# One column of ones beside each head's values, a fifth key and value tile, unread products in TensorE's gaps, and a new list of due times

## The chip, the cores and the metric

The kernel runs on one core of one Trainium2 chip. The metric is device microseconds (us) of one execution; the time of a kernel is the median of several runs. TensorE is written PE (its weight loads PEld), VectorE DVE, ScalarE ACT, GpSimd POOL and SyncE SP. All data is float32.

## The reference

Sixteen batches of 256 rows with 256 channels go through two blocks, 16 heads of 16 channels each. Cut to what matters:

```python
m = silu(mod) @ w_ada + b_ada                    # nine rows of shift, scale and gate per batch
h = ln(x) * (1 + sc_msa) + sh_msa                # self attention in windows of 128, rolled by 64
x = x + self_attn(h) * g_msa
h = ln(x) * (1 + sc_mca) + sh_mca                # cross attention to a context of 256 rows
scores = einsum('bqhd,bkhd->bhqk', q, k) / 4
top_s, top_i = top_k(scores, 16)                 # only the 16 largest scores of 256 are kept
x = x + (softmax(top_s) applied to v[top_i]) @ w_co * g_mca
h = ln(x) * (1 + sc_mlp) + sh_mlp
x = x + (silu(h @ w_a) * (h @ w_b) @ w_m2) * g_mlp     # hidden size 1024
# second block: x is the query, the context is normalised, shifted and scaled; plain attention
out = x + softmax(q k / 4) v @ Wp + bp
```

## The kernel before, in words

The work of one batch is cut into operations, each on one engine: a group of matmuls that fill one bank of PSUM, an activation over a bank, a vector operation, or a set of DMAs. `Plan.op` (line 195) only records them. Every operation has a due time from the table `DUE` (line 33): a whole number for the batch plus thousandths from the list of its stage. The stages are `start` (weights and conditioning), `self`, `prep` (context and queries of the cross attention), `topk`, `mlp` and `last` (the second block); the first two batches, and the last two, have lists of their own. `Plan.order` (line 231) sorts all operations by due time, lets none be due before what it depends on, and that sorted list is the program: each engine executes its operations in that order, SP its DMAs too. A small model of times in the same function serves one purpose in the kernel before, the choice of a buffer among those that will be free. `SWITCH` holds what the model adds where PE changes between its three ways of working: whole array (128), four tiles of 32 rows (32: scores) and four tiles of 32 columns (33: weighted values). `ISSUE`, `BEGIN`, `LAND`, `RATE` describe its DMAs.

In the middle of the run the due times overlap the batches: while batch b is in its cross attention, batch b+1 is in its self attention and batch b-1 in its feed forward and second block. Only the first batches (nothing earlier to overlap with) and the last one differ. Batch 15 is split in two halves of 128 rows from its self attention on (`SPLIT`).

Names and lines that matter below:

- PE transposes an image of normalised rows (line 449), multiplies by weights (475, 511, 558, 888, 915), makes the scores (780 and 788 self, 827 cross, 932 and 944 second block) and the weighted values (581, in `weighted`).
- Lines 661 to 749 make the shift, scale and gate rows of the conditioning. Line 703, in `ada_columns`, multiplies a block of weights by `condT`, 16 columns, one for each batch. Line 724 multiplies a bias by a weight.
- DVE finds the top 16 in two rounds of eight: MAX8 and MATCH_REPLACE8 at lines 846 and 854, then 866 and 871. It also finds row maxima (588), transposes blocks of 32 (538, 548) and divides (540).
- POOL multiplies exponentials with the kept places (875), ACT makes the exponentials (859, 612) and copies out of PSUM (497, 514, 528).
- `lower` (592) sends row maxima from one partition layout to another with eight small DMAs per half (line 605), on SP's queue.
- A value tile `v` holds for each head 16 channels and then 16 columns of ones (line 336), 32 columns in all (`NW`); the product at line 581 so makes the weighted values and, sixteen times over, the sum of the weights. Only the first of the sixteen sums is read, at line 540. The PSUM tiles are `W`, eight banks.

Of the kernel before, what the change touches and what calls it, by code (L numbers as in the profile page):

```python
# [12 lines left out]
ALU = mybir.AluOpType  # L13
# [3 lines left out]
P = 128  # L17
# [11 lines left out]
NW = 32  # L29
# [5 lines left out]
        -3027, -4397, -3471, -3599, -5098, -3376, -2645, -3084, -3618, -1977, -2570, -3085, -3359, -3247, -5174,  # L35
        -3588, -3596, -431, -695, -157, 8, -3035, -3444, -156, -402, -441, -3589, -3159, -3051, -3086, -3323, 86,
        -376, 159, 26, -148, 29, -158, 334, 377, 516, -136, -3437, 524, -402, 345, -448, 430, 1141, 1178, 1253, 540,
        1078, 1334, 228, -58, 443, -404, 1252, -71, 428, 1557, -57, 507, 841, 302, 299, 483, -230, -210, 96, -72,
        1354, 1417, 985, 1558, 1602, 445, 168, -27, 1258, 1342,
    ),  # L40
    "self0": (
        178, -1268, -3395, -1437, -1529, -1439, -5228, -2475, -56, -5103, -2746, -2747, -5249, -2746, -2706, -2925,
        -2729, -5250, -3573, -3327, -3037, -3016, -3187, -3023, -3039, -2555, -3040, -3039, 43, 140, -202, -1119,
        -1116, -910, -811, 145, -81, -38, -132, 17, 157, -1137, -808, -1336, -976, 254, -472, -362, -105, -363, 431,
        -718, -93,
    ),
    "prep0": (
        -2332, -1084, -15, -1103, -1963, 736, -1918, 514, 308, -228, -1334, -1335, 632, -769, 127, 694, -742,
    ),
    "topk0": (  # L50
        629, -11, 508, -65, -2495, -66, 291, 102, -772, 48, 291, 30, -776, 38, 290, 51, -2533, 90, 49, 468, 67, -2304,
        71, 30, 677, 698, -2305, 24, 93, -61, 708, -2254, 674, 702, -38, 789, -2249, 917, 909, 1267, 743, 1295, -125,
        63, -46, 39, -774, 42, -109, 705, -2577, 778, -97, 749, -2266, 745, -98, 745, -2463, 664, 654, 550, 850,
        -2335, 892, 809, -179, 967, -2308, 757, 903, -180, 969, -2327, 908, 719, -196, 1029, 681, 1073, 1237, 1296,
        847, 1335, 924, 961, 1061, 1120, 904, 914, 986, 1120, 686, 985, 978, 983, 924, 992, 1088, 787, 548, 1160, 893,
        998, 1181, 899, 1120, 1159, 1138, 1206, 1183, 998, 1008, 1106, 1004, 838, 1212, 950, 1085, 1192, 781, 1207,
        1244, 1255, 1232, 1293, 1161, 1159, 982, 890, 1096, 782, 1049, 1224, 900, 1184, 933, 1240, 894, 1216, 1140,
        1231, 886, 1224, 1217, 1032, 1206, 737, 1227, 1216, 752, 1198, 738, 1221, 1262, 858, 1287, 848, 1200, 1233,
        783, 1224, 810, 1326, 1299, 1222, 711, 1338, 723, 1099, 849, 1380,
    ),  # L60
    "self1": (
        -3478, -4042, -805, -510, -4612, -2278, -2316, -2237, -4112, -2262, -390, -1118, -3568, -3569, -1018, -2976,
        -3569, -395, -2322, -692, -1489, -1465, -682, -1456, -353, -1219, -1461, -1477, -1495, -1344, -161, -627,
        -165, -3303, -3251, -3334, -3335, -47, -57, 32, 68, 101, -299, -2850, -3108, -3088, -3253, -247, -186, 6,
        -1156, 83, -18, -16, 128,
    ),
    "prep1": (
        -4084, -4257, -17, 53, 102, -42, -411, 147, 218, 181, 36, 33, 206, -260, 510, 225, 282,
    ),
    "topk": (  # L70
        94, 53, 163, 160, 4, 121, -38, 55, -63, 145, -59, 66, 184, 59, -366, 67, 109, 463, -23, 372, 645, 559, 48,
        269, -313, 408, -161, 248, 353, 281, 408, -99, 373, -12, 392, 487, -206, 659, 476, 675, 182, 715, 463, -23,
        499, -47, -199, -24, 504, 82, 263, -22, 545, -475, 2, -451, 531, -453, 268, -421, -453, 561, 667, 565, 225,
        -487, 599, 775, 405, 592, 438, 668, 782, 652, -599, 692, 711, 781, 421, 836, 643, 846, -287, 927, 656, 739,
        712, 799, 836, 747, 417, 768, 859, 606, -19, 673, 566, 625, 195, 477, 684, 541, 942, 30, 1043, 790, 757, 902,
        26, 1047, 722, 784, 775, 756, 905, 863, 693, 718, 757, 907, 775, 1097, 1077, 1166, 825, 1182, 849, 956, 790,
        947, 751, 946, 791, 945, 879, 915, -152, 1008, 1103, 943, 792, 993, 874, 992, 1055, 390, 1120, 1069, 979, 955,
        -104, 1070, 1107, 1011, 972, 968, 1130, 1088, 993, 1010, 633, 1117, 1113, 1176, 1065, 1114, 964, 1201, 391,
        1238, 706, 1108,
    ),  # L80
    "self": (
        -1722, -443, -1198, -804, -2008, -1876, -1546, -1510, -950, -1210, -765, -667, -1033, -1065, -675, -624,
        -1069, -679, -1276, -593, -1090, -1091, -1115, -1012, -430, -1599, -1523, -1474, -1475, -1556, -865, -440,
        -308, -386, -445, -600, -603, -212, -219, -461, -1332, -185, -208, -478, -361, -315, -362, -158, -384, -446,
        -1376, -94, -423, -188, -953,
    ),
    "prep": (
        -23, 5, -310, -291, 112, 73, 257, -32, -1133, -1111, -1134, -3, -291, 405, 25, -209,
    ),
    "last": (  # L90
        1047, 1071, 1127, 1163, 1124, 1206, 712, 1303, 932, 999, 1381, 866, 2035, 1757, 1739, 1723, 2103, 2108, 2222,
        2149, 1885, 2182, 2205, 2121, 1997, 2108, 2080, 2268, 1996, 2015, 2066, 2065, 2014, 2284, 2287, 2028, 2226,
        1991, 2271, 2366, 2356, 2353, 2354, 2141, 1901, 2213, 2403, 1838, 1963, 2116, 2117, 2437, 2000, 2148, 2379,
        2458, 1833, 2404, 1968, 1877, 2530, 2091, 1631, 2565, 1630, 2532, 2446, 2359, 1777, 2068, 2559, 1500, 1410,
        2598, 2600, 2353, 2406, 2302, 2304, 2658, 2404, 2403, 2194, 2680, 2764, 2475, 2722, 2485,
    ),
    "mlp": (
        1494, 1306, 703, 702, 1361, 1433, 838, 1532, 1486, 1250, 1255, 1513, 1352, 1542, 1571, 1599, 1480, 869, 876,
        1488, 1420, 1529, 1359, 1415, 1520, 1197, 863, 1541, 1052, 1568, 1365, 1567, 1554, 1160, 1057, 1670, 1621,
        1724, 1029, 1709, 1814, 1620, 1616, 1553, 1150, 633, 1853, 1121, 1875, 1826, 1793, 1880, 1776, 869, 1898, 941,  # L100
        1609, 1300, 1303, 1625, 1530, 1560, 1531, 1525, 1829, 947, 932, 1677, 1535, 625, 1615, 624, 1989, 1963, 1766,
        1664, 893,
    ),
    "self15": (
        -1970, -648, -1706, -864, -1672, -2110, -1485, -1035, -2085, -1469, -710, -1217, -976, -689, -810, -1331,
        -670, -962, -412, -567, -648, -649, -677, -545, -509, -518, -239, -893, -998, -432, -907, -216, -458, -322,
        -1198, -169, -191, -594, -651, -564, -606, -158, -189, -224, -1271, -89, -174, -108, -1155, -2020, -1743,
        -493, -117, -97, -514, -47, -175, -176, -85, -148, -226, 106, 111, 32, 9, -666, -439, -29, -481, -571, -549,
        253, 149, -73, 249, -74, 317, 269, 257, 330, 323, 162, 60, -269, -4, 69, 211, 72, -4, 335, 413, 434, -56, 352,
    ),  # L110
    "prep15": (
        -81, -120, 34, -136, -399, 69, -211, -438, -39, -1166, -1149, 17, -568, -1106, 38, -400, 459, 424, 409, 523,
        9, 546, 533, 14,
    ),
    "topk15": (
        56, -306, 25, 48, 170, -288, -9, -86, 110, 142, 112, 97, 206, -87, -313, -87, 122, -241, 178, 233, 297, 268,
        152, 238, 161, 510, -5, 154, 322, 369, 534, 580, 153, 151, 106, 269, 215, 671, -599, 572, 189, 878, 421, 389,
        377, 441, 88, 404, 251, 461, 73, 489, 390, 507, 589, 157, 364, -324, -18, 360, 490, -68, 738, 554, 513, 534,
        578, 832, 559, 505, -196, 599, 743, 650, 535, 499, 563, 652, -223, 1019, 1046, 1048, 420, 1209, 601, -563,
        -608, 726, 1012, -512, -647, -604, 898, -605, 551, -517, 984, 745, 436, 884, -224, 763, 575, 340, 1090, 997,  # L120
        -677, 920, 398, 1144, 1115, 972, 782, 454, 1116, 1148, 831, 863, -1632, 1114, 1162, 1194, 1272, 498, 473,
        1296, 1040, 1022, 362, 880, 1006, 963, 452, 1229, 1234, 993, 476, 989, 1113, 1042, 435, 1169, 1195, 990, 981,
        423, 1117, 1009, 1223, 410, 579, 1334, 835, 1047, 1087, 363, 1359, 1297, 1249, 461, 706, 1356, 1052, 1417,
        1140, 1200, -360, 990,
    ),
    "last15": (
        -1505, 17, -219, 55, 280, 1060, 1078, 1157, 1267, 1164, 1161, 1306, 483, 994, 987, 629, 1631, -1051, 1973,
# [51 lines left out]


class Op:
    __slots__ = ("tag", "eng", "cost", "hold", "own", "kb", "emit", "due", "mode", "takes", "uses", "after", "start", "end", "n")


class Plan:
# [910 lines left out]
```

## Time and profile before

| | |
|---|---|
| runs | 1363.39, 1363.4 and 1395.84 us, median 1363.4 |
| the profiled execution | 1365.2 us, of which its span (first to last instruction) is 1363.1 |
| mean granted PE clock | 0.981 of full speed |
| busy in the span | PE 97%, PEld 76%, DVE 89%, ACT 74%, POOL 75% |
| from 220 to 1180 us, each 80 us | PE 79.5 to 80.0 busy, DVE 75.4 to 76.1 |
| first batch's first cross scores (line 827) | 58.2 us |
| last batch's first cross scores | 1208.7 us |

PE's busy time is modelled, because its matmuls are pipelined; a start of one matmul to the start of the next tells more than its length. A matmul of float32 shows as two records here, a transpose as one.

### The profile page before, as it was taken

The numbers are of one execution on the slowest core, as the hardware profiler recorded it, in microseconds if no ns is written. First come the engines' busy times: TensorE is split into PE (matmuls) and PEld (weight loads), VectorE is DVE, ScalarE is ACT, GpSimd is POOL, SyncE is SP. The second block draws the span as 40 slices with busy tenths as digits, with TensorE's granted clock in tenths as the row PEclk, the third lists the DMA queues.
The fourth block names the chain that finished last, engine by engine and source line by source line (L and its number), as shares of the span: only waits on it lengthen the run. The fifth ranks groups of instructions, "written<-read, shape, count | busy, mean of one in ns | idle before, by whom it ended". The sixth has DMA issues, their size and how long they took to land.

```text
span 1363.1 us, 38514 instructions
## 1 busy us (share of the span) xinstructions
PE 1327.1 (97%) x13464; PEld 1040.8 (76%) x13464; DVE 1216.9 (89%) x4357; ACT 1014.4 (74%) x2359; POOL 1026.4 (75%) x1552
## 2 busy tenths in 40 slices
PE   8699999999999999999999999999999999999996
PEld 6466787878778787877878787787878777787875
DVE  3699999999999999999999999999999999998734
ACT  4256778877777878777787878778787877877773
POOL 2456887878788787878878787787878787878752
PEclk9788999999999999999999999999999999999998
DMA  5412000101000010100001010001101000000000
GB/s 158 147 53 58 18 25 18 40 18 41 16 20 25 19 40 18 41 17 18 25 22 37 17 41 18 18 25 22 36 18 41 25 18 25 26 2 10 10 2 18
DMA packets 64161, 42.44 MB, mean 31 GB/s; under 512 B 37764, under 2 KB 56752, under 8 KB 63712
## 3 DMA queue, kind: packets, MB, share of 16 engines
q1 hardware_dynamic: 63967, 39.99, 10.9%
q8 instruction: 107, 1.75, 0.5%
q14 instruction: 87, 0.70, 0.2%
HBM read 35.14 MB, written 4.29 MB: 29 GB/s over the span
## 4 chain that ended last, share of the span: by engine, by line
PE 87%; DVE 5%; POOL 2%; DMA 2%; SPq 1%; issue 1%; ACT 1%; ACTq 0%; POOLq 0%; DVEq 0%
PE W L888 17%; PE W L475 11%; PE W L581 11%; PE W L525 8%; PE W L915 7%; PE W L511 6%; PE W L558 6%; PE W L944 5%; PE W L932 5%; PE W L827 5%; PE W L449 3%; PE W L788 3%; PE W L780 2%; DVE rest L854 1%; DVE rest L871 1%
## 5 line engine op out<-in xcount | busy, mean ns | idle before, releaser
L875 POOL TENSOR_TENSOR prT<-rest,prT 128x512 f32<-128x512 f32 x256 | 325.7, 1273 | 63.5 <-DVE rest L871 49.8
L859 ACT ACTIVATE prT<-W,ntop 128x256 f32<-128x256 f32 x512 | 216.8, 510 | 76.0 <-POOL ntop L848 64.3
L588 DVE TENSOR_REDUCE nm<-W 128x2 f32<-128x512 f32 (+1 forms) x384 | 236.9, 681 | 28.1 <-PE W L932 16.0
L888 PE MATMUL W<-xT,w_L_xcond_w_m 128*128 128x256 f32 (+1 forms) x1088 | 249.0, 375 | 1.5 <-ACT xT L463 1.5
L612 ACT ACTIVATE pTO<-W 128x512 f32<-128x512 f32 (+1 forms) x392 | 200.5, 613 | 62.0 <-PE W L944 37.6
L888 PEld LDWEIGHTS W<-xT,w_L_xcond_w_m 128*128 128x128 f32 x1088 | 189.1, 190 | 57.0 <-ACT pTO L612 10.9
L854 DVE MATCH_REPLACE8 rest<-top,W 128x256 f32<-128x256 f32 x512 | 208.2, 416 | 0.2 <-issue 0.2
L871 DVE MATCH_REPLACE8 rest<-top,rest 128x256 f32<-128x256 f32 x512 | 205.5, 409 | 0.0
L846 DVE MAX8 top<-W 128x8 f32<-128x256 f32 x512 | 187.0, 417 | 14.7 <-PE W L827 14.5
L866 DVE MAX8 top<-rest 128x8 f32<-128x256 f32 x512 | 187.3, 410 | 0.0
L525 PE MATMUL W<-ident,prT 128*128 128x128 f32 x1024 | 144.4, 279 | 11.1 <-POOL prT L875 11.1
L528 ACT ACTIVATE pTT<-W 128x512 f32<-128x512 f32 x256 | 148.4, 621 | 8.8 <-PE W L525 8.7
L541 POOL TENSOR_TENSOR on<-tr,rec 128x128 f32<-128x128 f32 (+1 forms) x162 | 71.0, 443 | 98.6 <-DVE rec L540 98.2
L525 PEld LDWEIGHTS W<-ident,prT 128*128 128x128 f32 x1024 | 120.3, 143 | 32.6 <-POOL prT L875 14.6
L905 POOL TENSOR_TENSOR mb<-ma,mb 128x256 f32<-128x256 f32 (+1 forms) x136 | 94.7, 697 | 62.7 <-ACT mb L903 50.6
L538 DVE STREAM_TRANSPOSE tr<-W 128x256 f32<-128x256 f32 (+1 forms) x162 | 79.2, 490 | 48.1 <-PE W L581 40.1
L915 PE MATMUL W<-w_L_xcond_w_m,h 128*128 128x256 f32 x512 | 113.8, 380 | 0.0
L581 PE MATMUL W<-pTO,v 128*32 128x128 f32 (+1 forms) x2112 | 108.1, 329 | 2.3 <-ACT pTO L612 2.0
L915 PEld LDWEIGHTS W<-w_L_xcond_w_m,h 128*128 128x128 f32 x512 | 95.9, 190 | 13.6 <-POOL prT L875 0.8
L908 POOL TENSOR_TENSOR h<-h,mb 128x256 f32<-128x256 f32 (+1 forms) x136 | 94.8, 697 | 8.3
L581 PEld LDWEIGHTS W<-pTO,v 128*32 128x32 f32 x2112 | 57.8, 111 | 42.6 <-ACT h L907 10.2
L903 ACT ACTIVATE mb<-W,half 128x256 f32<-128x256 f32 (+1 forms) x136 | 69.6, 513 | 9.7 <-PE W L888 8.4
(126 smaller groups left out, 2675.2 us busy)
## 6 DMA issues: line engine op xcount, KB each, us to landing
gate<-gates SPq DMA_DIRECT2D x48, 256.0 KB
q<-nmT SPq DMA_DIRECT2D x480, 1.0 KB
cx<-in_ctx_dram SPq DMA_DIRECT2D x19, 256.0 KB
cx<-in_ctx_dram SPq DMA_DIRECT2D x104, 32.0 KB
rest<-in_L_xcond_w_ada_dram SPq DMA_DIRECT2D x9, 256.0 KB
x<-in_x_dram SPq DMA_DIRECT2D x16, 128.0 KB
x<-in_x_dram SPq DMA_DIRECT2D x32, 64.0 KB
w_L_xcond_w_m<-in_L_xcond_w_m_dram SPq DMA_DIRECT2D x1, 2048.0 KB
```

What stands on the lines that cost most here:

```text
L525: nc.tensor.transpose(w.t[:, ts(n, P)], flat[:, ts(n, P)], ident)
L581: nc.tensor.matmul(po.t[ds(NW * j, NW), ds(q0, nq)], v.t[:, kt, 8 * m + 2 * j + a, :], pT.t.rearrange("p n q -> p (n q)")[:, ds(part, nq)] ...
L588: op("DVE", 0.61, lambda j=j, s=s: nc.vector.tensor_reduce(nm.t[:, k, ds(j, groups, step=4)], s.t.rearrange("p (g k) -> p g k", g=groups), ...
L612: op("ACT", 0.24 + q * 0.0005, lambda s=s, pT=pT: nc.scalar.activation(pT.t.rearrange("p n q -> p (n q)")[:, :q], s.t[:, :q], AF.Exp), r=[ ...
L846: nc.vector.max(top.t[:, a, 0:8], s.t[:, ts(a, L)])
L854: nc.vector.match_replace(rest.t[:, a, :], top.t[:, a, 0:8], s.t[:, ts(a, L)], TAKEN)
L859: nc.scalar.activation(pr.t[:, a, :], s.t[:, ts(a, L)], AF.Exp, bias=ntop.t[:, a:a + 1])
L866: nc.vector.max(top.t[:, a, 8:16], rest.t[:, a, :])
L871: nc.vector.match_replace(rest.t[:, a, :], top.t[:, a, 8:16], rest.t[:, a, :], TAKEN)
L875: op("POOL", 1.25, lambda: nc.gpsimd.tensor_tensor(pr.t, rest.t, pr.t, ALU.mult), r=[rest, pr], w=[pr])
L888: nc.tensor.matmul(w.t[:, :q], w_m1.t[:, c, ds(n0, P)], xT.t[:, c, :q], start=c == 0, stop=c == NCC - 1)
L915: nc.tensor.matmul(pp.t[:, ts(k, C)], hs[f].t[:, ts(k, P)], w_m2.t[:, f, :], start=f == 0, stop=f == NHC - 1)
```

## The change

Seven edits, in one diff:

1. The value tile has one column of ones instead of 16: 17 columns for each head. The product at line 581 then writes 17 of the 32 partitions of each tile of the array.
2. Five tiles instead of four for keys (`k2`) and for values (`v`).
3. `filler`: matmuls of the identity with four copies of itself, 128x512, into a free bank that nobody reads. `Plan.order` puts them where its model sees PE idle for more than 0.8 us, as many as 0.43 us each go into the gap less 0.3.
4. `condT` has 128 columns, of which 16 are used and the others are zero; the products at line 703 get 128 columns each.
5. The model's cost of such a product falls from 1.7 to 0.9, and of DMAs `ISSUE` rises from 0.47 to 0.53 and `LAND` falls from 1.0 to 0.4.
6. All lists in `DUE` are new, so every engine's order is.
7. The slice of the gate rows' product takes the 16 used columns of `condT`.

In the order that results, 38 such unread matmuls stand on PE: 11 ahead of the first batch's first cross scores, 11 more ahead of the third batch's, and 16 after the last batch's last ones. There are none between. The counts of all other instructions stay, but for the filling of a fifth value tile and of `condT`.

```diff
-ISSUE, BEGIN, LAND, RATE, OPEN = 0.47, 0.9, 1.0, 320.0, 8
+IDLE, FILLER = 0.8, 0.43
+ISSUE, BEGIN, LAND, RATE, OPEN = 0.53, 0.9, 0.4, 320.0, 8
...
             o.start = t
+            if o.eng == "PE" and t - free["PE"] > IDLE and free["PE"]:
+                n = int((t - free["PE"] - 0.3) / FILLER)
+                ok = [z for z in slots["W"] if z[0] < free["PE"] + 0.3]
+                if ok and n:
+                    at, slot = ok[-1]
+                    slots["W"].remove((at, slot))
+                    insort(slots["W"], (t, slot))
+                    o.fill = self.tiles["W"][slot], n
...
+            if o.fill:
+                self.filler(*o.fill)
             o.emit()
...
-        "k2": (4, [P, NCC, 2, L]), "v": (4, [P, NT, NH, NW]), "gate": (3, [P, 2, C]), "nm": (4, [P, NT, 32]), "nmT": (4, [P, NT, 32]),
+        "k2": (5, [P, NCC, 2, L]), "v": (5, [P, NT, NH, DH + 1]), "gate": (3, [P, 2, C]), "nm": (4, [P, NT, 32]), "nmT": (4, [P, NT, 32]),
...
-        nc.gpsimd.memset(t[:, :, :, DH:NW], 1.0)
+        nc.gpsimd.memset(t[:, :, :, DH:], 1.0)
...
+    def filler(t, n):
+        for _ in range(n):
+            nc.tensor.matmul(t, ident, ident.unsqueeze(1).to_broadcast([P, 4, P]), start=True, stop=True)
...
-                    nc.tensor.matmul(po.t[ds(NW * j, NW), ds(q0, nq)], v.t[:, kt, 8 * m + 2 * j + a, :],
+                    nc.tensor.matmul(po.t[ds(NW * j, DH + 1), ds(q0, nq)], v.t[:, kt, 8 * m + 2 * j + a, :],
...
-    condT = fixed("condT", [P, NCC, B])
+    condT = fixed("condT", [P, NCC, P])
+    nc.vector.memset(condT.t, 0.0)
...
-                    nc.tensor.matmul(pm.t[:, ts(m, B)], w.t[:, c, ts(m, P)], condT.t[:, c, :], start=c == 0, stop=c == NCC - 1)
-        op("PE", 1.7, emit, r=[w, condT], w=[pm], mode=128)
+                    nc.tensor.matmul(pm.t[:, ts(m, P)], w.t[:, c, ts(m, P)], condT.t[:, c, :], start=c == 0, stop=c == NCC - 1)
+        op("PE", 0.9, emit, r=[w, condT], w=[pm], mode=128)
```

## The prediction

> **What bounds the kernel now.** I read the page first, then the busy times by stretch, then the starts of single instructions on PE and DVE, and last the order that each list of due times gives each engine.
>
> ```profile
> span 1363.1 us, 38514 instructions
> PE 1327.1 (97%) x13464; PEld 1040.8 (76%) x13464; DVE 1216.9 (89%) x4357; ACT 1014.4 (74%) x2359; POOL 1026.4 (75%) x1552
> PEclk9788999999999999999999999999999999999998
> ```
>
> PE looks full, but the digits of its granted clock dip at both ends. By stretch (PE, PEld, DVE, ACT, POOL busy, then clock, DMA share, GB/s):
>
> ```profile
> 0.00:20.00 20.00, 14.14 (x83) 11.89 (x87) 5.55 (x30) 7.73 (x15) 7.27 (x21) 1.00 0.70 220
> 20.00:40.00 20.00, 19.64 (x202) 16.28 (x197) 9.40 (x27) 11.04 (x23) 0.73 (x2) 0.81 0.29 83
> 40.00:60.00 20.00, 17.80 (x153) 11.86 (x152) 12.19 (x35) 3.40 (x7) 11.61 (x16) 0.85 0.59 203
> 60.00:80.00 20.00, 10.96 (x60) 7.50 (x60) 18.75 (x78) 8.67 (x19) 10.54 (x16) 0.58 0.18 55
> 540.00:620.00 80.00, 80.00 (x844) 63.19 (x840) 75.80 (x270) 62.90 (x145) 64.18 (x96) 1.00 0.10 25
> 1340.00:1363.00 23.00, 15.41 (x247) 11.21 (x240) 9.08 (x24) 6.78 (x13) 2.83 (x5) 0.87 0.10 25
> ```
>
> Three regimes. To 60 us PE and a chain of DMAs set the pace, at a clock of 0.81 to 0.85. From 60 us DVE does (18.75 of 20 us), while PE waits for the first top 16. From about 180 us PE is never idle. The first MAX8 of each batch starts at 59.4, 116.3, 182.4, 261.6 us and then every 79.2 (79.16 where undisturbed), the last at 1209.9; the end is 153.2 us after that. So a gain comes from the first 182 us, from the last 153, or from what PE does in each 79.2.
>
> **The sum, against the profiled execution's span of 1363.1.** Its own time is 1365.2, 2.1 more than the span and 1.8 more than the median of the runs, 1363.4; I take the median as span plus 0.3.
>
> *Narrow values.* The rows of the weighted values:
>
> ```profile
> L581 PE MATMUL W<-pTT,v 128*32 128x128 f32 x2048 | 71.1, 277 | 0.9 <-ACT pTT L528 0.8
> L581 PEld LDWEIGHTS W<-pTT,v 128*32 128x32 f32 x2048 | 54.4, 110 | 26.0 <-ACT pTT L528 16.8 <-ACT pTO L612 4.3 <-issue 1.8
> ```
>
> A matmul's length goes by its moving columns, which stay. In the raw starts four matmuls of 128 columns begin every 0.109 us whatever is loaded beside them, so a load of 0.110 us is hidden; only the first of a group is not: the second four begin 0.240 us after the first in a group of 256 columns, then every 0.216. That is 0.024 us for 32 columns, 0.011 less for 17 in proportion. There are 134 groups: -1.5 us (ends 0 and -3.2, the whole 0.024).
> The Trainium skill, "TensorE: Matmul & The Clock Gate", section "LDWEIGHTS (loading the stationary operand)", prices a load by its columns over 1.2, so 12.5 ns less for 15 columns; 4160 loads would by that give an estimated 52 us. The rows show them under other matmuls, so I do not take it. A load that became longer than the 0.109 us between matmuls would show at once; that is a rival below.
>
> *Wider products of the conditioning, ones, fifth tiles.* Eight records at line 703 with 16 columns take 1.06 us at full clock; eight of 128 columns (line 525) take 1.04. Filling condT is one DVE memset, by the row of line 334 (four in 0.33 us) about 0.1, in DVE's 1.78 us of idle ahead of 2.92 us. POOL's filling of the ones, 1.98 us, shrinks; it then sat idle until 6.77. The tiles issue nothing. Together 0; without that cover, 0.1.
>
> *The middle.* From the third batch on I counted in both orders how often PE changes between whole array, row tiles and column tiles: 32 times a batch in both, and equally often for each pair (10 from rows to whole, 6 for each of three pairs, 2 for the other two). The last matmul before a change is followed 0.309 instead of 0.217 us later, whichever pair it is. Same matmuls, same changes: 0 us for thirteen batches. No fillers stand there. Ends: an order that makes PE wait 0.5 us a batch, +6.5; the 0.2 us that single batches differ in before, -2.6.
>
> *First 58 us.* In PE's timeline (start, length):
>
> ```profile
> 12.09 5.30 PE L475 MATMUL W<-xT,w_L_xcond_w_qkv 128*128 128x256 f32 x16 [1.60 <-DMA w_L_xcond_w_qkv<-in_L_xcond_w_qkv_dram]
> ...
> 33.79 2.48 PE L581 MATMUL W<-pTO,v 128*32 128x128 f32 x32
> ...
> 58.24 1.14 PE L827 MATMUL W<-k,q 32*128 32x512 f32 x8 [0.56 <-ACT q L486]
> 68.24 1.11 PE L525 MATMUL W<-ident,prT 128*128 128x128 f32 x4 [8.86 <-POOL prT L875]
> ...
> 80.35 1.08 PE L581 MATMUL W<-pTO,v 128*32 128x128 f32 x32
> ```
>
> The same 32 records of line 581 take 2.48 us at 33.8 and 1.08 at 80.4: half clock. A filler has two records of 512 columns, at 0.216 us per 256: 0.864 us, twice the 0.43 that the model gives it. (1) The qkv weights move from SP's 13th DMA to its 9th (0.58 us each), with 512 KB less ahead, so their wait of 1.60 ends; next late is the image of the rows, which ACT has at 11.6, and two fillers end at about 12.1. So the product starts no earlier, but 24 records of qkv take 24 x 0.217 = 5.2 us at full clock instead of 6.96: -1.8. (2) From the self scores at 31.5 to the end of the projection at 48.1 PE took 16.6 us. In the new order at full clock: scores 1.1, four fillers 3.5, values 1.0, two groups of scores 2.1, a wait for ACT's 2.1 us of exponentials to about 8.9 after the start, values 1.0, then DVE and POOL (0.7+0.2+0.6+0.4 and hand-overs) and a projection of 1.8: 13.9, so -2.7. (3) Two more fillers stand before the query product, one behind it. They cover waits of about 1.4 and 0.55: +0.7. (4) Line 724 for Wp now stands ahead of the transposes that the first cross scores need, and its weights leave SP behind 1 MB of w_m2. Three MB from 35 us at the 203 GB/s of 40 to 60 us land near 50, where PE arrives near 49: +0.8. Sum -3.0. Ends: -4.5 (no wait at 3 and 4) and +2 (no better clock, fillers at half clock 1.7 us each).
>
> *58 to 182 us.* DVE's work in the orders, at the starts of its rows (0.333 us a MAX8, 0.40 a replacement with its load, 0.615 a maximum): between the first MAX8 of batches 0, 1 and 2 it is 53.9 and 63.5 before, 54.0 and 63.0 after. The times were 56.9 and 66.1, so 3.0 and 2.6 idle. The second group of cross scores now stands ahead of the first transposes, which ends 1.1 us of that idle; 0.5 us less work. Eleven fillers sit in stretches where PE had 26 us of waits and half clock. -1.5 (ends -4, most of the idle gone, and +2).
>
> *The end.* After the last cross scores PE has 130.8 us of work before and 130.2 after by these rows, of 154.4. The last idle stretches:
>
> ```profile
> 1333.97 0.44 PE L449 MATMUL W<-ident,xn 128*128 128x128 f32 x2 [1.69 <-POOL xn L437]
> 1334.96 1.28 PE L475 MATMUL W<-xT,w_L_xcond_Wq 128*128 128x128 f32 x8 [0.55 <-ACT xT L463]
> 1336.79 3.44 PE L932 MATMUL W<-k,q 32*128 32x256 f32 x32 [0.55 <-ACT q L497]
> 1345.44 1.08 PE L581 MATMUL W<-pTO,v 128*32 128x128 f32 x32 [2.03 <-ACT pTO L612]
> 1358.35 0.70 PE L558 MATMUL W<-w_L_xcond_Wp,oT 128*128 128x256 f32 x2 [1.11 <-DVE oT L548]
> ```
>
> Into these go 1, 2, 2, 4, 2 and 3 fillers (and 2 earlier, into 0.93 us): two are 1.7 us where the wait is 0.55. I walk from the end of the last feed-forward product, 1329.3. The query product starts 6.8 us later instead of 5.7; the scores 9.4 instead of 7.5, but take 2.0 us instead of 3.44. DVE's two blocks of maxima then start 1.0 late, and eight DMAs behind each carry that on. Four fillers (3.5) stand where exponentials need 2.2, which costs 1.0 on the last scores; the last values end 28.6 instead of 27.3. DVE and POOL take 1.75, and three fillers (2.6) let the last projection start at 31.2 instead of 29.1. With a full clock it is 0.3 shorter: +1.8, and +0.7 at the two earlier: +2.5. Ends -3 (the fillers hidden and the clock's 3 us gained) and +9 (half of 13.8 us of fillers and what they delay).
>
> Sum: -1.5 + 0 - 3.0 - 1.5 + 2.5 = -3.5, a span of 1359.6, a time of **1359.9 us**, own range 1354 to 1366.
>
> The skill's rule on the clock, same page, "The HAM clock gate (the "warmup" mystery)", is that about 3.4 us of idle halve the clock and as much of activity restores it. In 20 to 40 us the clock is 0.81 with PE busy 19.64, so what counts as activity is narrower than busy. By the rule fillers win all of the half clock; whether identity matmuls count no run here shows.
>
> **Rivals.** (A) *Fillers on the chain, slower.* Place: the last 35 us and the first 58. For: 16 x 0.864 = 13.8 us at the end, against idle of 1.69, 0.55, 0.55, 2.03, 1.11, and the model believes half the price. Against: each stands where something is waited for, and the clock rises. With the ends +9 and +2, and the rest as above: 1363.1 - 1.5 - 1.5 + 2 + 9 = 1371.1, time 1371. It decides from an overrun of 3.5 us in sum above mine. (B) *A wait in every batch.* For: new order, and DVE has only 2.8 of 79.2 us free. Against: DVE's counts and PE's changes agree. 0.8 us a batch is +10.4: 1370. Related, and the one way beyond 2%: loads of 17 columns, 68 bytes apart, slower than 109 ns; 0.05 us for each of 8 starts in 100 groups is +40, 1400. (C) *Both ramps shrink*: -4.5, -4, -3 and -1.5 make 1350. For: all DVE idle is a wait for PE. Against: the overruns. (D) *The clock dips stay* in spite of the fillers: +2 at the start, fillers at 1.7 us, end +6, rest as above: 1368. For: half clock with PE busy at 32 us.
>
> **How the numbers follow.** Forecast 0.56, A 0.14, B 0.10 (0.05 of it beyond 2%), C 0.13, D 0.07. The range reaches past C and A: 1349 to 1374. A measurement of this kernel tells about 2% (27 us) from no change; faster by that needs the two ramps to lose over a third of the 76 us that they hold beside PE's own work (182 less 130 counted, 154.4 less 130.8): 0.04. Slower: 0.07, B's tail and an unforeseen wait. Within: 0.89.
>
> **What would show it.** Right: starts of MAX8 near 56.4 and 178 us, then 79.2 apart; clock 1.0 from 20 to 60 us; the last feed-forward product ending some 35.6 us before the end instead of 33.8; filler records 0.43 us apart in pairs. Wrong: batches over 79.7 apart (B), first scores later than 58 (A, D), an end stretch under 150 us (C), or second starts at line 600 later than 0.24 us (the loads).

## The result and the profile after

The changed kernel takes 1368.8 us, median of five runs (1367.1 to 1369.4), beside 1363.4 before: 1.0042 times as long, with an interval of 1.0026 to 1.0058. That is 5.4 us slower, where 3.5 us faster were forecast. It is within 2%, but the runs do not overlap: those of before lie between 1361.0 and 1363.4, but for one of 1395.84, which was a slow one and does not count in the ratio.

The page of the profile after, its span, the first row of busy times and the granted clock in 40 slices:

```profile
span 1366.0 us, 38751 instructions
PE 1343.3 (98%) x13540; PEld 1039.7 (76%) x13540; DVE 1218.4 (89%) x4358; ACT 1012.8 (74%) x2359; POOL 1024.2 (75%) x1553
PEclk9999999999999999999999999999999999999999
```

Two things stand side by side: the clock no longer dips, and PE is busy for 16.2 us more. The same by stretch (PE, PEld, DVE, ACT, POOL busy, then clock, DMA share, GB/s):

```profile
0.00:20.00 20.00, 16.13 (x119) 11.44 (x119) 6.43 (x33) 7.14 (x14) 5.64 (x22) 1.00 0.66 201
20.00:40.00 20.00, 19.59 (x224) 13.14 (x219) 11.95 (x35) 9.48 (x19) 0.62 (x1) 1.00 0.26 76
40.00:60.00 20.00, 17.83 (x119) 12.47 (x114) 9.76 (x33) 4.37 (x9) 11.86 (x17) 1.00 0.53 165
60.00:80.00 20.00, 17.91 (x143) 12.58 (x142) 20.00 (x82) 11.77 (x26) 7.61 (x11) 0.83 0.43 147
540.00:620.00 80.00, 80.00 (x830) 62.82 (x823) 76.78 (x274) 62.60 (x144) 64.14 (x96) 1.00 0.10 25
1340.00:1363.00 23.00, 21.25 (x270) 13.27 (x262) 9.52 (x24) 6.78 (x13) 2.82 (x5) 1.00 0.07 19
```

The first row says less of the clock than it seems: the clock's record begins at 9.0 us here (at 15.4 before), and the time ahead of it counts as full.

From 20 to 60 us the clock is 1.00 where it was 0.81 and 0.85. All the same, the first MAX8 of the first batch ("first scores" below) starts at 58.7, only 0.7 earlier than before. PE's timeline (start, length) shows where the rest went:

```profile
12.86 3.62 PE L494 MATMUL W<-xT,w_L_xcond_w_qkv 128*128 128x256 f32 x16
34.95 1.07 PE L600 MATMUL W<-pTO,v 128*17 128x128 f32 x32
51.40 1.10 PE L744 MATMUL W<-w_L_xcond_Wp,h 128*128 128x256 f32 x4 [1.89 <-DMA w_L_xcond_Wp<-in_L_xcond_Wp_dram]
53.07 1.98 PE L355 MATMUL W<-ident 128*128 128x512 f32 x4
57.57 1.14 PE L847 MATMUL W<-k,q 32*128 32x512 f32 x8
```

The qkv product takes 3.62 us where it took 5.30, and the 32 records of weighted values 1.07 where they took 2.48: the full clock. Then PE waits 1.89 us for the weights Wp, which the transposes behind it do not need but stand behind in PE's order, and two fillers (L355) follow.

The rows of the weighted values, all executions of the kernel together (busy, mean ns of one, idle before):

```profile
L600 PE MATMUL W<-pTT,v 128*17 128x128 f32 x2048 | 68.6, 274 | 1.0 <-ACT pTT L547 0.9
L600 PEld LDWEIGHTS W<-pTT,v 128*17 128x17 f32 x2048 | 52.0, 97 | 26.2 <-ACT pTT L547 12.9 <-ACT prT L879 4.3 <-ACT pTO L631 4.3
```

A load takes 97 ns where it took 110. And the end, PE's timeline again:

```profile
1333.35 0.44 PE L468 MATMUL W<-ident,xn 128*128 128x128 f32 x2 [0.45 <-POOL xn L456]
1333.98 1.98 PE L355 MATMUL W<-ident 128*128 128x512 f32 x4 [0.19 <-ACT pTO L631]
1335.80 1.05 PE L494 MATMUL W<-xT,w_L_xcond_Wq 128*128 128x128 f32 x8
1336.69 1.88 PE L355 MATMUL W<-ident 128*128 128x512 f32 x4
1338.50 2.01 PE L952 MATMUL W<-k,q 32*128 32x256 f32 x32
1348.68 3.70 PE L355 MATMUL W<-ident 128*128 128x512 f32 x8
1355.38 1.88 PE L355 MATMUL W<-ident 128*128 128x512 f32 x4
1358.18 2.84 PE L355 MATMUL W<-ident 128*128 128x512 f32 x6
1360.86 1.03 PE L577 MATMUL W<-w_L_xcond_Wp,oT 128*128 128x256 f32 x4
```

Of the bracketed waits of before (1.69, 0.55, 0.55, 2.03 and 1.11 us) 0.45 us is left, and fillers of two records, 0.9 us each, stand there, one to four in a place. A wait that is covered too long is not listed as a wait: it is read from what starts later. How long the same order waits without fillers is shown with the first experiment.

By stretch, from starts of the first MAX8 of a batch, in us:

| | before | after | difference | forecast |
|---|---|---|---|---|
| start to first batch | 59.4 | 58.7 | -0.7 | -3.0 |
| first batch to third | 123.0 | 122.9 | -0.1 | -1.5 |
| third to fifteenth, median of 12 gaps | 79.16 | 79.31 | +0.15 each | -0.09 each |
| fifteenth to last | 76.4 | 77.8 | +1.4 | part of the end |
| last to the end of the span | 153.3 | 154.5 | +1.2 | +2.5 in all |

The last row is called the last stretch below. The twelve gaps of the third row add up to 951.1 us before and 952.1 after, so to +1.0 and not to twelve times 0.15, because single gaps of before are longer than the median, up to 80.04.

The spans differ by 2.9. The medians differ by 5.4 because the profiled execution of before was one of its longer ones (1365.2, 1.8 above its median) and that of after one of its shorter (1367.8, 1.0 below).

### The profile page after: what moved, and what is told of

The parts are those of the page before. It is cut to its first block, busy times and chain, and to the rows that moved or that the text cites. A ratio compares the mean times of both kernels' runs of the same rounds, so it can differ in the third digit from the quotient of the medians.

```text
span 1366.0 us, 38751 instructions
## 1 busy us (share of the span) xinstructions
PE 1343.3 (98%) x13540; PEld 1039.7 (76%) x13540; DVE 1218.4 (89%) x4358; ACT 1012.8 (74%) x2359; POOL 1024.2 (75%) x1553
## 4 chain that ended last, share of the span: by engine, by line
PE 91%; DVE 3%; POOL 2%; issue 1%; ACT 1%; DMA 1%; SPq 1%; DVEq 0%; POOLq 0%; ACTq 0%
PE W L908 18%; PE W L494 12%; PE W L600 11%; PE W L935 8%; PE W L544 8%; PE W L577 5%; PE W L530 5%; PE W L964 5%; PE W L847 5%; PE W L952 4%; PE W L468 3%; PE W L808 3%; PE W L800 2%; PE W L355 2%; DVE top L866 1%
## 5 line engine op out<-in xcount | busy, mean ns | idle before, releaser
L879 ACT ACTIVATE prT<-W,ntop 128x256 f32<-128x256 f32 x512 | 212.4, 500 | 45.4 <-POOL ntop L868 38.6
L547 ACT ACTIVATE pTT<-W 128x512 f32<-128x512 f32 x256 | 143.8, 627 | 15.4 <-PE W L544 15.2
L544 PE MATMUL W<-ident,prT 128*128 128x128 f32 x1024 | 136.8, 275 | 2.6 <-POOL prT L895 1.2
L544 PEld LDWEIGHTS W<-ident,prT 128*128 128x128 f32 x1024 | 117.3, 141 | 20.9 <-POOL prT L895 4.0
L560 POOL TENSOR_TENSOR on<-tr,rec 128x128 f32<-128x128 f32 (+1 forms) x162 | 70.7, 443 | 56.9 <-DVE rec L559 56.5
L600 PE MATMUL W<-pTO,v 128*17 128x128 f32 (+1 forms) x2112 | 106.6, 325 | 0.6 <-ACT pTO L631 0.3
L600 PEld LDWEIGHTS W<-pTO,v 128*17 128x17 f32 x2112 | 53.2, 97 | 44.9 <-ACT mb L923 18.5
L418 POOL TENSOR_TENSOR x<-x,gated 128x512 f32<-128x512 f32 (+1 forms) x49 | 59.9, 1223 | 32.1 <-ACT gated L417 32.1
```

The source lines that it names most:

```text
L544: nc.tensor.transpose(w.t[:, ts(n, P)], flat[:, ts(n, P)], ident)
L600: nc.tensor.matmul(po.t[ds(NW * j, DH + 1), ds(q0, nq)], v.t[:, kt, 8 * m + 2 * j + a, :], pT.t.rearrange("p n q -> p (n q)")[:, ds(part, ...
L879: nc.scalar.activation(pr.t[:, a, :], s.t[:, ts(a, L)], AF.Exp, bias=ntop.t[:, a:a + 1])
```

## The experiments

Ratios are to runs of the kernel before on the same chip.

**No fillers.** The condition `IDLE` is never met; the order of everything else stays.

```diff
-IDLE, FILLER = 0.8, 0.43
+IDLE, FILLER = 1e9, 0.43
```

> The changed kernel without its 38 fillers; order, tiles and narrow values stay. Theory F (the fillers stand on the chain: 13.8 us of them in the last 35 us, and 2.74 us of them at 120 us ahead of a product that VectorE waits for): taking them out wins more than the half clock that comes back, so 1363 to 1366, with the stretch behind the last feed-forward product at 35 to 36 us where it is 37.3, and second batch to third at 66 where it is 67.9. Theory O (the new order itself is the slower one, and the fillers pay for themselves by the clock): 1370 to 1374, with the clock at half speed again around 35 to 45 and 100 to 110 us and first scores at 59 or later.

Measured: 1361.7 (1357.6 to 1367.3), ratio 0.9990 (0.9978 to 1.0003). So the fillers cost 7 us, theory F, and more than F had. The last stretch is 149.1 instead of 154.5, and second batch to third 66.9 instead of 67.9. But the clock fell only to 0.991 in the profiled execution and to 0.991 to 0.998 in the others, where the kernel before has 0.981 to 0.991: most of the clock was not the fillers' work. In the profiled execution the wait for Wp was 3.25 us; the clock's record then has half speed from 52.9 to 59.7, the query product behind the wait takes 3.78 us where it took 1.89 in the changed kernel, and first scores were late, at 61.2.

At the end PE of this kernel waits as follows, at the places of the fillers:

```profile
1335.83 0.44 PE L468 MATMUL W<-ident,xn 128*128 128x128 f32 x2 [0.45 <-POOL xn L456]
1336.82 1.28 PE L494 MATMUL W<-xT,w_L_xcond_Wq 128*128 128x128 f32 x8 [0.55 <-ACT xT L482]
1338.65 2.17 PE L952 MATMUL W<-k,q 32*128 32x256 f32 x32 [0.55 <-ACT q L516]
1349.57 2.52 PE L600 MATMUL W<-pTO,v 128*17 128x128 f32 x32 [0.64 <-ACT pTO L631]
1358.29 0.70 PE L577 MATMUL W<-w_L_xcond_Wp,oT 128*128 128x256 f32 x2 [1.11 <-DVE oT L567]
```

The new order has already cut the two long waits, 1.69 to 0.45 and 2.03 to 0.64. Four fillers take 3.70 us where 0.64 is waited, three take 2.84 where it is 1.11. From the end of the last feed-forward product to the end of the span it is 33.8 us before, 37.3 in the changed kernel and 31.9 without fillers.

The place at 120 us that was named beforehand, first PE's timeline of the changed kernel, then DVE's, then the same instruction of DVE without fillers:

```profile
120.08 2.74 PE L355 MATMUL W<-ident 128*128 128x512 f32 x6
122.75 1.07 PE L600 MATMUL W<-pTT,v 128*17 128x128 f32 x32
```

```profile
123.96 0.45 DVE L557 STREAM_TRANSPOSE tr<-W 128x256 f32<-128x256 f32 x1 [1.23 <-PE W L600]
```

```profile
126.60 0.45 DVE L557 STREAM_TRANSPOSE tr<-W 128x256 f32<-128x256 f32 x1
```

Three fillers run for 2.74 us; the weighted values start behind them, and DVE waits 1.23 for these. Without fillers it does not wait there, and second batch to third is 1.0 shorter.

**The true price.** The planner counts 0.87 us for a filler, so it places 14 instead of 38. (The expectations say 13 here and 6 further on; the traces have 28 and 14 records, so 14 and 7 fillers.)

```diff
-IDLE, FILLER = 0.8, 0.43
+IDLE, FILLER = 0.8, 0.87
```

> The changed kernel with one number changed: the planner counts 0.87 us for a filler, which is what two records of 512 columns take, instead of 0.43, so 13 fillers stand where 38 stood, and each fits the wait that the planner foresees. Theory F: most of the overrun goes and most of the clock stays: 1363 to 1366, the stretch behind the last feed-forward product 34.5 to 36 us. Theory O: as slow as the changed kernel or slower, 1368 to 1371.

Measured: 1359.3, ratio 0.9974 (0.9964 to 0.9984), 4 us below the range that F expected. The last stretch is 149.3.

**Fillers of half the length.** All 38 in their places, each 256 columns, which takes the 0.43 us that the planner counts.

```diff
-            nc.tensor.matmul(t, ident, ident.unsqueeze(1).to_broadcast([P, 4, P]), start=True, stop=True)
+            nc.tensor.matmul(t[:, :2 * P], ident, ident.unsqueeze(1).to_broadcast([P, 2, P]), start=True, stop=True)
```

> The changed kernel with its 38 fillers in their places, each of 256 moving columns instead of 512, so that it takes the 0.43 us that the planner counts. Theory F: it was the length, so as with 13 fillers at the true price: 1358 to 1361, clock 0.996 or more. Rival: it is their number and the banks that they take: 1365 to 1369.

Measured: 1359.7, ratio 0.9974 (0.9965 to 0.9984). With length and price in agreement the loss is gone, from either side; number and banks of the fillers make no difference that these runs can tell.

**No fillers at the end.** The kernel of 14 fillers without the last seven.

```diff
-            if o.eng == "PE" and t - free["PE"] > IDLE and free["PE"]:
+            if o.eng == "PE" and t - free["PE"] > IDLE and 0 < free["PE"] < 1000:
```

> The kernel of 13 fillers without the 7 fillers behind the last cross scores, so 6 in the first 115 us alone. Theory T (at the end fillers win nothing: 145.5 us from the last first MAX8 to the end without any, 145.7 with 7): the same as with 13, 1359, the stretch 145 to 146. Rival: the clock falls at the end and costs 1 to 2 us: 1360 to 1361, the stretch 147.

Measured: 1359.3, ratio 0.9975 (0.9965 to 0.9985), last stretch 149.0. Theory T: at the end fillers win nothing. (The 145.5 and 145.7 us in this and a later expectation count from a mark some 3.6 us later than the first MAX8; from that it is 149.1 and 149.3.)

**Wp first.** One due time moves the 1 MB of `w_m2` behind Wp on SP's queue; all 38 fillers stay.

```diff
-        1361, 1433, -617, 241, -4201, -4071, -4075, -1670, -5305, 155, -5644, 370, 185, 144, 482, 255, -5546, 101,
+        1361, 1433, -617, 241, -4201, -4071, -4075, -1670, -5305, 155, -5644, 370, 256, 144, 482, 255, -5546, 101,
```

> The changed kernel (38 fillers) with one due time moved, so that the 1 MB load of w_m2 leaves SyncE behind the load of Wp and not ahead of it. Theory W: the wait of 1.89 us for Wp at 49.5 us goes, and first scores come 1 to 1.9 us earlier, 57 instead of 58.7; the time falls by as much, 1367 to 1367.8. Rival: the row of the query product that comes behind is late anyway, or the fillers there take up the room: no change, 1368.8.

Measured: 1363.9, ratio 1.0010 (1.0002 to 1.0019): 4.8 us less by the medians, 4.4 by the ratios, from one number and more than theory W had. PE's timeline of this kernel, the two groups that stood at 51.40 and 57.57:

```profile
48.48 1.10 PE L744 MATMUL W<-w_L_xcond_Wp,h 128*128 128x256 f32 x4
54.66 1.14 PE L847 MATMUL W<-k,q 32*128 32x512 f32 x8
```

The wait is gone and first scores are 2.9 us earlier. 0.9 of it stood already ahead of the wait: the group before it (line 723) starts at 47.42 instead of 48.34, and the clock's record begins at 7.0 instead of 9.0 us, which the order of two later loads does not explain. So 2.0 of the 2.9 are the wait's. In the profiled executions second batch to third and the end are unchanged; the gap from first to second batch is 53.7 instead of 55.0.

**Narrow values alone**, in the kernel before.

```diff
-        "k2": (4, [P, NCC, 2, L]), "v": (4, [P, NT, NH, NW]), ...
+        "k2": (4, [P, NCC, 2, L]), "v": (4, [P, NT, NH, DH + 1]), ...
...
-                    nc.tensor.matmul(po.t[ds(NW * j, NW), ds(q0, nq)], v.t[:, kt, 8 * m + 2 * j + a, :],
+                    nc.tensor.matmul(po.t[ds(NW * j, DH + 1), ds(q0, nq)], v.t[:, kt, 8 * m + 2 * j + a, :],
```

> The kernel before with the values of 17 columns and nothing else of the change. The prediction's term: 134 groups, 0.011 us less each, is 1.5 us off, 1361.9 where the kernel before is at 1363.4, batches 79.1 apart. Its rival: loads of 17 columns 68 bytes apart are no cheaper on the path, 1363.4 and 79.2. If the narrow loads cost something, over 1364.

Measured: 1360.7, ratio 0.9987 (0.9978 to 0.9996), or 1.8 us less. The median gap between batches is 79.06 beside 79.16: 0.10 us a batch, where the forecast's 0.011 us for each of some eight groups makes 0.09.

**The old due times with everything else.**

> The whole change but its due times: the changed kernel with the lists of due times of the kernel before. The planner then puts in 47 fillers, 20 of them in one place while VectorE finds the first top 16. Theory F: 2 to 6 us slower than the kernel before, 1365 to 1369. Theory O: the clock stays up and the old order keeps its place: 1358 to 1362.

(Edit: the lists of `DUE` are those of the kernel before.) Measured: 1372.1, ratio 1.0064 (1.0052 to 1.0076), above what F expected. The price of 0.43 is as wrong in the old order: the 20 fillers in one place stretch first batch to second from 56.9 to 62.6, and the last stretch from 153.3 to 158.0.

**The old middle in the new kernel.** Five lists of `DUE` go back, in the kernel with the price 0.87; `xn`, `gate` and `gw` have one tile more and `k2` one less.

> The kernel of 13 fillers (planner's price 0.87) with the five lists of due times for the middle batches (topk, self, prep, last, mlp) taken from the kernel before; for that order it has one more tile of gw, gate and xn and one less of k2. Theory M: the new middle order costs 0.25 us a batch (0.14 where the fourth product of a group waits for a bank that ScalarE still reads, 0.07 in another group, the rest in what stands first and last between changes of mode), so batches 79.05 to 79.1 apart instead of 79.3, 3.3 us less over 13 batches, 1356. Rival: the 0.25 comes with the fifth tiles or the narrow values in this stream and not with the order: 79.3 and 1359.

Measured: 1406.3, ratio 1.0319 (1.0305 to 1.0332). As a time this missed both expectations: where lists of two orders meet, work waits (first batch to second 66.9, second to third 75.1, fifteenth to last 91.9, last to end 163.0, some 49 us in all), and the planner places 32 fillers in this mixture. As a measure of the middle it holds: the median gap is 79.06, with the same narrow values whose gap in the new order is 79.31. So theory M, 0.25 us a batch from the order. The rival, the fifth tiles, falls by the kernel of wide products below: the old order with five tiles of both has 79.06 too. By the mean of the twelve gaps it is less, 79.34 beside 79.16 with narrow values alone, 0.18 us a batch and 2.1 in all, because single gaps of the old order are longer, up to 79.93.

Where it sits is seen in the changed kernel's timeline of PE, of a group of 16 scores of the second block and of ACT beside it:

```profile
612.59 1.29 PE L964 MATMUL W<-q,k 32*128 32x256 f32 x16
```

```profile
612.23 0.47 ACT L923 ACTIVATE mb<-W,half 128x256 f32<-128x256 f32 x1
```

and such a group in the kernel before:

```profile
613.54 1.15 PE L944 MATMUL W<-q,k 32*128 32x256 f32 x16
```

The group writes four banks at once. In the kernel of 14 fillers, where single starts were read, three of the first four products start within 14 ns of each other and the fourth 0.15 us later, just after an ACT read of a bank ends. The trace does not number the banks; in the plan that the kernel makes, the fourth bank is one that an activation of the feed forward read last. A group of line 952 loses 0.07 a batch; about 0.04 is left for what stands first and last between changes.

**A bank freed earlier?** In the kernel "all three" below, one exponential of ACT moves behind the activation that frees a bank.

```diff
-        481, 484, -784, 619, 548, 515, -916, 422, -1710, 592, -1579, 550, 606, 478, 534, 483, -1159, 618, 618, -1566,
+        481, 484, -784, 619, 548, 515, -916, 422, 520, 592, -1579, 550, 606, 478, 534, 483, -1159, 618, 618, -1566,
```

> The kernel of all three with one instruction moved on ScalarE in each of the batches 1 to 14: the activation that frees the bank of a feed-forward product now goes ahead of an exponential of the top 16 weights instead of behind it. Theory B: the 0.14 us that the fourth product of a group waits for that bank goes, batches 79.15 apart instead of 79.3, 1.8 us less. Rival: ScalarE's later exponential is then waited for, or the wait moves to the next group: 79.3 or more, no gain.

Measured: 1360.3, ratio 0.9981 (0.9972 to 0.9990), gaps 79.53. The remedy failed. The same group now takes 1.43 us from start to start instead of 1.22, which is the whole difference of the gaps (79.53 beside 79.32): the planner hands out banks by its own times, and gave the group a bank that the delayed exponential holds. That a bank is waited for fits both; that this exchange would end it was wrong.

**All three: price, no fillers at the end, Wp first.**

> The changed kernel with what the earlier runs point to: the planner's price of a filler at 0.87, none behind the last cross scores, and the load of w_m2 behind that of Wp. If the three add up: the 1359.3 of the kernel with 6 fillers less 1 to 3 us for the wait for Wp (it waited in some executions and not in others), so 1356 to 1358, first scores at 55.5 to 57, the last stretch at 145.5. If filler price and load order remove the same wait: 1359.

Measured: 1357.4, ratio 0.9963 (0.9951 to 0.9976), first scores at 55.9, the last stretch 149.2. They add up.

**Wp first and no filler at all.**

> The changed kernel with w_m2 behind Wp and without any filler. What fillers win by the clock, once they fit: 2.4 us slower than the kernel of all three, as 1361.7 stood against 1359.3, so 1359 to 1360, with half clock again in two or three places of the first 115 us. If the fillers at their true price only covered the wait for Wp: equal to it.

Measured: 1357.0, ratio 0.9957 (0.9945 to 0.9969). The expectation of a slower kernel fell, and the other held: with Wp in its place the fillers win nothing that these runs can tell, where with Wp late they won 2.4 us (1359.3 beside 1361.7). So they had covered the wait for Wp. Its clock by stretch:

```profile
20.00:40.00 20.00, 18.47 (x236) 12.94 (x239) 12.10 (x35) 9.49 (x19) 0.92 (x2) 1.00 0.35 90
40.00:60.00 20.00, 17.63 (x101) 12.00 (x97) 13.00 (x48) 6.79 (x15) 12.10 (x20) 1.00 0.62 186
```

PE is busy for less of these 40 us than before, without one filler, and the clock is full. Something else in the change had won it there; the next two runs ask what.

**Wide conditioning products in the old order**: old due times, no fillers, everything else of the change. Beside narrow values alone it differs by the products of 128 columns, by the fifth tiles, which issue nothing, and by the model's constants of edit 5, by which the planner chooses buffers.

> Everything of the change but the new due times and the fillers: narrow values, fifth tiles and the conditioning products of 128 columns, in the order of the kernel before. Beside the kernel before with narrow values alone (0.9987 of the kernel before) it differs by the wider products. Theory C (the wider products keep the clock up where those of 16 columns let it fall; the fillers do not matter): clock 1.0 from 20 to 60 us, first scores at 55 to 56.5 instead of 57.3 to 59.4, 0.997 of the kernel before or 1359. Theory N (the order does it): half clock between 32 and 46 us as before, 0.9987 or 1361.

Measured: 1358.6, ratio 0.9967 (0.9954 to 0.9979), the time of theory C. The clock of this kernel:

```profile
20.00:40.00 20.00, 18.96 (x230) 14.84 (x230) 9.42 (x28) 11.84 (x25) 0.62 (x1) 1.00 0.22 68
40.00:60.00 20.00, 15.79 (x152) 10.20 (x150) 13.16 (x41) 3.96 (x8) 10.37 (x15) 0.98 0.63 211
```

and of narrow values alone, with products of 16 columns in the same order:

```profile
20.00:40.00 20.00, 19.45 (x228) 15.02 (x223) 9.78 (x29) 11.67 (x24) 0.62 (x1) 0.91 0.26 79
40.00:60.00 20.00, 15.15 (x148) 9.98 (x146) 13.66 (x43) 3.18 (x7) 10.94 (x16) 1.00 0.63 209
```

These two executions do not show where the gain lies. First scores come at 58.1 with the wide products, outside of what theory C had, and at 57.3 with the narrow ones; over the whole span the clock is 0.985 beside 0.989. The one is the slowest of its kernel's six runs (1360.9), the other the fastest of eleven (1359.4).

**Narrow conditioning products in the new order**: the kernel with Wp first and no filler, with `condT` back at 16 columns.

> The kernel without fillers and with the late w_m2 (1357.0), with the conditioning products back at 16 columns. Theory C: half clock again between 20 and 60 us, first scores 1 to 3 us later than 54.5, 1358.5 to 1360. Theory N: the order keeps the clock up: 1357, clock 0.997, first scores at 54.5.

Measured: 1359.1, ratio 0.9978 (0.9965 to 0.9991), clock:

```profile
0.00:20.00 20.00, 13.41 (x87) 11.50 (x91) 5.89 (x30) 7.16 (x14) 5.68 (x22) 1.00 0.65 199
20.00:40.00 20.00, 18.45 (x243) 12.93 (x239) 12.79 (x35) 9.49 (x19) 0.62 (x1) 1.00 0.25 73
40.00:60.00 20.00, 17.83 (x123) 13.11 (x124) 12.59 (x44) 6.06 (x13) 12.22 (x19) 1.00 0.59 182
```

Both theories hold in part. The new order alone has full clock from 20 to 60 us (N), but the wide products are still worth about 2 us in either order (0.9987 to 0.9967 in the old, 0.9978 to 0.9957 in the new; each pair's intervals overlap a little). In the new order the place is seen, the first qkv product, with 128 columns and with 16:

```profile
11.75 3.75 PE L494 MATMUL W<-xT,w_L_xcond_w_qkv 128*128 128x256 f32 x16 [0.66 <-ACT xT L482]
```

```profile
11.68 5.49 PE L494 MATMUL W<-xT,w_L_xcond_w_qkv 128*128 128x256 f32 x16 [0.66 <-ACT xT L482]
```

The clock's record begins, at full speed, at 10.7 us with the wide products and at 15.3 with the narrow ones, and first scores come at 54.5 and 55.9. This is one execution of each. That the width did it, and not the moment at which the clock happened to rise, rests on the medians (1357.0 and 1359.1).

**The old order as a whole**, with the narrow values, wide products and 14 fillers at the true price in the first 62 us.

> All due times of the kernel before, with the narrow values, and with fillers at the price 0.87 in the first 62 us alone: 4 before the first cross scores and 10 where PE waits 8.9 us for the first transposes. It tells what the new order is worth as a whole, beside the kernel with the new order, 6 fillers and the late w_m2. If the new order is worth its place: about 1359, slower than that kernel by 2 to 3 us (its ramp and end win more than the 3.3 us that its middle loses). If the old order with the same help is as good: 1356 to 1357.

Measured: 1357.8, ratio 0.9960 (0.9948 to 0.9972), the same as the new order's 1357.4. What the new order wins at the end (149.2 beside 153.9) it loses in the middle (the twelve gaps add up to 952.5 beside 950.7, and 77.5 beside 76.3 follow) and up to the third batch (176.3 beside 174.9).

## Why the prediction was wrong

The step that failed most is the credit in the term of the end: fillers at twice the model's price were set against a full clock that they would buy, and came out at +2.5 us. The runs show 38 of them as 7 us of net cost, because the clock mostly stays up without them (0.991 to 0.998 over the span, beside 0.996 to 0.998 with them). Term (4) of the first 58 us, the wait for Wp, failed in size: +0.8 forecast, 4.4 to 4.8 us measured. "Same matmuls, same changes: 0" for the middle measured +2.1 us; it left out, as far as the times show, the wait for a fourth bank. And "the median as span plus 0.3" became the span plus 2.8 (1366.0 and 1368.8), which is 2.5 of the 8.9 us between 1359.9 and 1368.8.

The runs make a ladder from one kernel to the other, one step at a time:

| step | ratio to before | us, times 1363.4 |
|---|---|---|
| values of 17 columns | 0.9987 | -1.8 |
| conditioning products of 128 columns | 0.9967 | -2.7 |
| new order, Wp first | 0.9957 | -1.4 |
| `w_m2` ahead of Wp | 0.9990 | +4.5 |
| 38 fillers at the price of 0.43 | 1.0042 | +7.1 |

The steps add up to +5.7 (1.0042 times 1363.4 is 1369.1). The third is less than its own uncertainty; its parts are seen in the traces. In another order of steps the shares move: a late Wp costs 4.5 us without fillers, but with 7 fitting ones 1.9 (1359.3 beside 1357.4; 1.6 by the ratios). The second step holds the fifth tiles and the model's constants too.

*Narrow values*, forecast -1.5: right. The second starts of a group moved from 0.240 to 0.227 us, and the load lost 13 ns. The Trainium skill's page "TensorE: Matmul & The Clock Gate", section "LDWEIGHTS (loading the stationary operand)", gives a load as its columns over 1.2, by which 15 columns are an estimated 12.5 ns; the 110 and 97 ns agree with this difference, not with the lengths (27 and 14 ns by the same rule). The 52 us that it would have made in all stay hidden, as the forecast held.

*Wider products*, forecast 0: a miss by some 2 us. Their price was rightly read (1.06 us for eight records of 16 columns, 1.05 for eight of 128). That they could change the clock for what stands around them was not asked; the new order shows that in one pair of executions, the old order does not.

*The middle*, forecast 0: the step that failed there is "same matmuls, same changes: 0". The changes are 32 in both orders, as counted. Not counted was that a group of four tiles needs four free banks in the same moment. By the mean of the gaps it is 0.18 us a batch, 2.1 in all, a quarter of what rival B asked for; that the wait is for a bank fits the times, but the remedy that was tried failed.

*First 58 us*, forecast -3.0, measured -0.7. The clock rose as forecast, but term (4) was mis-sized: Wp behind `w_m2` was put at +0.8, from 3 MB at 203 GB/s landing near 50 us. From 35 us until Wp's product could start at 51.4 the DMAs moved some 3.9 MB (239 GB/s). PE waited 1.89 in this execution (3.25 in that without fillers), first scores lost 2.0 and the median 4.4 to 4.8 us. First scores after 58, a sign of being wrong that the text names for rivals A and D, came true at 58.7, while the half clock of D did not.

*58 to 182 us*, forecast -1.5, measured -0.1. The fillers were taken to cover idle time; three of them at 120 us stood ahead of values that DVE needed, and second batch to third is 1.0 shorter without them.

*The end*, forecast +2.5, measured +2.6 with the gap before it, right by luck, as two errors cancel: fillers cost 5.4 there (154.5 to 149.1) and 0.3 in the gap, and the new order without them wins 4.2 (153.3 to 149.1) and loses 1.1 in the gap (76.4 to 77.5). Behind the last feed-forward product the text put the overrun at +1.8, from 33.8 to 35.6; it is 37.3 with fillers and 31.9 without, 5.4. The mechanism, fillers at twice the model's price, was in the text; rival A has its price and its place. What failed is the credit set against it: the full clock was booked as the fillers' gain, and at the end it is there without them: the record of the kernel without fillers is full from 111 to 1360 us. Without that credit the fillers are overrun, 7 us net.

*The base.* The gain of the first 58 us was counted on one profiled execution with a clock of 0.981. Of 29 later executions of the kernel before, the four with 0.981 took 1365.3 to 1365.8 us and the others, 0.983 to 0.991, 1360.9 to 1364.2. So nearly 2 us of the half clock that could be won were not there in the median execution.

What stays open: of the 4.2 us that the new order without fillers needs less at the end, 1.9 lie behind the last feed-forward product, where its long waits are shorter (0.45 and 0.64) and the scores take 2.17 us instead of 3.44 at half clock; the 2.3 ahead of it are not explained. Nor is it known which banks would have to be exchanged to free the middle of its wait.

## What to carry to other kernels

Before a planner fills idle time, its price for the filling must be the measured one; at half the true price gaps are overrun, and the profile then shows fewer waits and a longer kernel. Credit a better clock to an edit only after a run without that edit. One load placed ahead of another on a queue can cost more than the other edits beside it win (4.4 to 4.8 us here, beside 1.8, 2.7 and 1.4): ask of each transfer that was moved who needs the next one, and when.

## What the runs showed of the hardware

- PE was busy for 19.64 of the 20 us from 20 to 40 with a clock of 0.81 before, and for 18.47 with a clock of 1.00 with Wp first and no filler. So a busier PE did not have the better clock. Products of 16 and of 128 columns take as long, 1.06 and 1.05 us for eight at full clock; the kernel with those of 128 is about 2 us faster in either order. In the new order the record of the clock is full at 10.7 us with them and at 15.3 without, one execution each.
- In the clock's record of the profiled executions stretches at half speed last 3.4, 6.8, 10.2, 13.7 or 17.1 us, multiples of one step of 3.4. The Trainium skill's page "TensorE: Matmul & The Clock Gate", section "The HAM clock gate (the "warmup" mystery)", has a window of this length that runs freely, so that the same kernel meets it at another phase in each execution; the spread of 1357.6 to 1367.3 us of the kernel without fillers, beside 1367.1 to 1369.4 with them, agrees with that.
- Four filler records took 3.78 us at 4.1 us and 1.98 at 53 us, where the clock's record is full. The first lie ahead of the record's beginning at 9.0, so their half clock is read from their length.
- Behind waits of PE for Wp of 2.61, 3.00 and 3.25 us (7 fillers, half fillers, none) the record of the clock has half speed for 3.4, 3.4 and 6.8 us, and behind one of 1.81 us for POOL in the kernel of 14 fillers for 3.4; behind 1.89 us for Wp in the changed kernel it stays full. All are shorter than the 3.4 us of idle in the rule that the prediction quotes.
